# A planner that models the transfer queue, scores three tiles ahead, the mask on VectorE and the gate bias in column quarters

## The chip, the cores and the metric

One core of one Trainium2 chip runs the kernel. The metric is the device time of one execution in microseconds; of the kernel before there are three runs, median 474.86 us (474.11 to 476.41). One more execution was taken with the hardware profiler.

## The reference

Input X is 4 sequences of 1024 tokens with 256 features, all in float32. Four residual stages follow one another:

```python
x = x + attention(layernorm(x))      # causal, one head, scores / 16
x = x + ffn(layernorm(x))            # token shift, r = sigmoid, k = relu squared
x = x + state_space(x)               # own layernorm inside, gate silu(z)
x = x + ffn(layernorm(x))
# attention
Q, K, V = X @ Wq.T + bq, X @ Wk.T + bk, X @ Wv.T + bv
s = where(causal, -inf, Q @ K.T / 16);  out = softmax(s) @ V
# state_space: xz = xn @ W_in.T + b_in with xn = norm(x) * ln_g + ln_b
x_proj, z = split(xz);  z = silu(z)
B = x_proj @ W_B.T * mean(dt);  x_mean = causal convolution of B with a decay per state
y = (x_mean @ W_C.T + D_skip * x_proj) * z @ W_out.T + b_out
```

## The kernel before, in words

**Tiles.** A batch b has 8 tiles of 128 tokens; tile i = 8b + t runs over all 32. A half j = 2b + h holds four tiles, 512 tokens. Features lie in two blocks of 128 (KC = 2). Matmuls are float32, and the profile counts two instructions for each.

**Stages.** In attention every tile i has its values `pv` (L1061), its scores `sc` against all earlier tokens of the batch (L1089), a mask, the row minimum (`least`, DVE L1104; the scores carry a minus sign), the exponentials (`exponents`, ACT L1109), the turned exponentials `prT`, and the product `po` with the values (`weigh`, L1189, added to x at L1199). The mask is a bf16 matmul of an identity with a 128x128 mask into the diagonal block of the score tile, the last of the group (L1096). The first ffn (`mix1`, tag f) and the preparation of the state stage (`state_prepare`, tag h) run between the attention tiles, a batch half behind. Then come the gates of the state stage (`pz`), its inputs (`pb`), the convolution (`pc`, with sixteen shifted decay rows `hk` of 512 KB each loaded from DRAM), its outputs (`py`, `pyo`) and the second ffn (`mix2`, tag g).

**Turning.** Normalised rows have to be turned (tokens to columns). `by_dram` (L482) writes a half to DRAM (`rows_`), reads it back in four pieces (`blocks_`) and lets VectorE turn 32x32 blocks (L501); `turn_by_dram` (L1124) does it with the exponentials (`exps`, `pblocks`, L1146). Tiles with t of 0 or 1 in each batch are turned by TensorE instead (`turn`, L1158: 1 and 2 transposes into PSUM, then a copy). The first and last halves are turned by TensorE too.

**State weights.** `state_weights` (L819) multiplies W_in with ln_b for the gate bias: `pb_all`, 8 matmuls of one column each (L827), then adds b_in (L833), scales W_in by ln_g, and so on, in three steps in iterations 20 to 22.

**The order of the work.** The kernel sets the order of every engine by itself. TensorE's order is that of the calls of `unit` in the program text: the loop over i at the end gives in iteration i the scores of tile i+2, the values of i+3, first and second parts of the ffn, and `po` of tile i. All other work is given to class `Order` (L48) as `op` with a key, the keys that it needs, one or more ways (engine, cost in us, function) and a lag until its result can be used. `Order` walks along TensorE's units, keeps a model time, and as soon as an op's needs are in the model ready it goes to the offered list; the op with the earliest start, then the lowest rank, then the earliest ready time is emitted. A transfer is an op on SP (0.45 us) with a fixed lag (2.2 to 9 us), whatever else is under way. `behind(i)` (L995) is a need that holds the write of a half behind the last read of tile i's exponentials. `load(at, ...)` (L243) offers the loads of weights and tokens at a fixed model time. PSUM is two `pair` buffers (scores, `py`) and four `bank` buffers. 34 slots of SBUF are shared by most tiles.

```python
        start, _, _, n = min(
            (self._way(op)[1], op["rank"], op["time"], n) for n, op in enumerate(self.offered)
        )
```

Of the kernel before, what the change touches and what calls it, by code (L numbers as in the profile page):

```python
# [19 lines left out]
P = 128  # L20
# [16 lines left out]
RPAD = P + L  # L37
TURNED_BY_DRAM = 2
# [9 lines left out]
class Order:  # L48
# [8 lines left out]

    LAG = 0.15

    def __init__(self):  # L60
        self.now = self.at = 0.0
        self.free = {}
        self.ready = {}
        self.waiting = []
        self.offered = []
        self.psum = {"bank": [0.0] * 4, "pair": [0.0] * 2}

    def _offer(self, op):
        if all(k in self.ready for k in op["needs"]):
            op["time"] = max([self.at] + [self.ready[k] for k in op["needs"]]) + op["delay"]  # L70
            self.offered.append(op)
            return True
        return False

    def _done(self, key, time):
        if key is not None:
            self.ready[key] = time
            self.waiting = [op for op in self.waiting if not self._offer(op)]

    def _way(self, op):  # L80

        return min(
            (
                (max(op["time"], self.free.get(e, 0.0)) + c, max(op["time"], self.free.get(e, 0.0)), e, f)
                for e, c, f in op["ways"]
            ),
            key=lambda w: w[0],
        )

    def _first(self):  # L90

        if not self.offered:
            return math.inf, None
        start, _, _, n = min(
            (self._way(op)[1], op["rank"], op["time"], n) for n, op in enumerate(self.offered)
        )
        return start, n

    def _step(self):
        self.at, n = self._first()  # L100
        op = self.offered.pop(n)
        end, _, engine, emit = self._way(op)
        self.free[engine] = end
        emit()
        if op["frees"]:
            heapq.heappush(self.psum[op["frees"]], end + self.LAG)
        self._done(op["key"], end + op["lag"])

    def op(self, key, needs, *ways, frees=None, delay=0.0, lag=LAG, rank=0):

        op = dict(key=key, needs=needs, ways=ways, frees=frees, delay=delay, lag=lag, rank=rank)
        if not self._offer(op):
            self.waiting.append(op)

    def known(self, key, time):
        self._done(key, time)

    def unit(self, key, cost, needs, emit, takes=None):

        while True:  # L120
            while self._first()[0] <= self.now:
                self._step()
            missing = [k for k in needs if k not in self.ready]
            full = takes and not self.psum[takes]
            if not missing and not full:
                start = max([self.now] + [self.ready[k] for k in needs])
# [5 lines left out]
            else:  # L132
                assert self.offered, (key, missing, takes, self.psum)
# [5 lines left out]
        emit()  # L139
        self.now += cost  # L140
        self._done(key, self.now + self.LAG)

    def finish(self):
        while self.offered:
            self._step()
        assert not self.waiting
# [11 lines left out]
def hybrid_kernel(  # L158
# [84 lines left out]
    def load(at, key, *transfers, after=(), queue="SP", lag=3.0):  # L243
        o.known(f"t{at}", at)
        for k, emit in enumerate(transfers):
            last = k == len(transfers) - 1
            o.op(key if last else None, [f"t{at}", *after], (queue, 0.5, emit), lag=lag, rank=3)
# [59 lines left out]
    load(6.0, "xl2", *tokens(0, 4, 8), lag=4.0)  # L307
# [35 lines left out]

    mask_f = const.tile([P, P], F32, tag="mask_f", name="mask_f")
    make_causal_mask(nc, mask_f, MASKED)
    steps_i = const.tile([P, FINE], mybir.dt.int32, tag="steps_i", name="steps_i")
    nc.gpsimd.iota(steps_i, pattern=[[1, FINE]], base=0, channel_multiplier=0)
    mask = const.tile([P, P], BF16, tag="mask", name="mask")
    ident_b = const.tile([P, P], BF16, tag="ident_b", name="ident_b")
    steps = const.tile([P, 2, FINE], F32, tag="steps", name="steps")  # L350

    def later_constants():
        nc.vector.tensor_copy(mask, mask_f)
        nc.vector.tensor_copy(ident_b, ident)
        nc.vector.tensor_copy(steps[:, 0, :], steps_i)
        nc.vector.tensor_scalar_mul(steps[:, 1, :], steps[:, 0, :], float(FINE))
# [17 lines left out]
    def normalized(  # L374
        key, b, h, needs, dst, names, second=False, by_hand=False, after=(), spans=((0, NH),)
# [9 lines left out]
        rank = 0 if key[0] == "g" else 1  # L385
# [67 lines left out]
        for n in range(NH):  # L453
            o.op(f"{key}.st{n}", [needs[n]], ("DVE", 0.53, partial(stats, n)), rank=rank)
        for n0, n1 in spans:
# [4 lines left out]
                ("DVE", 0.08 * k, partial(variances, n0, n1)), rank=rank,  # L460
# [7 lines left out]
                ("DVE", 0.08 * k, partial(shifts, n0, n1)), rank=rank,  # L468
            )
            for n in some:  # L470
# [4 lines left out]
                    rank=rank,  # L475
                )
        parts = [f"{key}.xn{n}" for n in range(NH)]
        if not by_hand:
            by_dram(key, xn, parts + list(after), dst, names)
        return xn, parts, rs, mrs  # L480

    def by_dram(key, xn, needs, dst, names):  # L482
# [24 lines left out]
        late = 3.6 if key[0] == "g" else 5.0  # L507
        o.op(f"{key}.w", needs, ("SP", 0.45, write), lag=2.2, rank=2)
        for j in range(P // GRP):
            o.op(f"{key}.r{j}", [f"{key}.w"], ("SP", 0.45, partial(read, j)), lag=late, rank=2)  # L510
# [56 lines left out]
    class Mix:  # L567
# [4 lines left out]
        def prepare(self, j, by_hand=False, after=()):  # L572
# [9 lines left out]
                after=after,  # L582
# [59 lines left out]
        def gates(self, j, g):  # L642
            key = f"{self.tag}{j}"
            if g == 0:
# [6 lines left out]
                f"{key}.r{g}", [f"{key}.pr{g}"],  # L651
# [5 lines left out]
        def values(self, j, g):  # L657
# [24 lines left out]
            def store():  # L682
# [3 lines left out]
                f"{key}.rv{g}", [f"{key}.r{g}", f"{key}.pv{g}"], ("DVE", dve(HALF), gate),  # L686
# [3 lines left out]
            if last:  # L690
                o.op(None, [f"{key}.x{g}"], ("SP", 0.45, store), rank=3)

        def last_values(self, j, n, d0, d1):
# [12 lines left out]
            def finish():  # L706
# [11 lines left out]
                None, [f"{key}.r{n // 2}", f"{key}.pv{n}.{d0}"], ("DVE", 2 * dve(d1 - d0), finish),  # L718
# [56 lines left out]
    def decay_table():  # L775
# [29 lines left out]
        for q in range(4):  # L805
            o.op(f"r{q}", ["dec"], ("SP", 0.8, partial(write, q)), rank=3)
# [3 lines left out]
    load(40.0, None, partial(nc.sync.dma_start, r_dram[:, :P], zeros))  # L810
# [8 lines left out]
    def state_weights():  # L819
# [3 lines left out]

        def biases():
            for e in range(2 * KC):
                for c in range(KC):
                    nc.tensor.matmul(  # L827
                        pb()[:, e : e + 1], lhsT=w_in[:, c, ts(e, P)], rhs=lnb[:, c : c + 1],
                        start=(c == 0), stop=(c == KC - 1),
                    )  # L830

        def add_biases():
            nc.vector.tensor_add(b_all, pb()[:, : 2 * KC], bin_c)  # L833
# [8 lines left out]
        o.unit("pb_all", 2.0, ["w_in", "ln", "bin", "dsk"], biases, "bank")  # L842
        o.op("b_all", ["pb_all"], ("DVE", 0.2, add_biases), frees="bank")
# [11 lines left out]

        o.unit("pt_wx", 4 * TURN, ["w_in0", "w_in1"], turn, "bank")
# [138 lines left out]
    def behind(i):  # L995


        if not 0 <= i < NB * NT:
            return []
        return [f"e{i}.r{P // GRP - 1}" if i % NT >= TURNED_BY_DRAM else f"e{i}"]  # L1000

    xa_rows, xa, q, v, pr, prT, sums = {}, {}, {}, {}, {}, {}, {}

    def attend_prepare(j, by_hand=False):
# [5 lines left out]
            after=behind(NH * j - 5), spans=((0, 2), (2, NH)) if j == 0 else ((0, NH),),  # L1010
        )

    def attend_transpose(j, spans=((0, NH),)):
# [4 lines left out]
        for n0, n1 in spans:  # L1018
            for c in range(KC):
                def emit(c=c):  # L1020
# [54 lines left out]
    def scores(i):  # L1075
# [4 lines left out]
        qh, vh, keys = q[2 * b + h], v[2 * b + h], [xa[2 * b + k] for k in range(h + 1)]  # L1080
# [4 lines left out]
        def emit():  # L1085
            for k in range(h + 1):
                w = min(HALF, nk - k * HALF)
                for c in range(KC):
# [5 lines left out]
                        stop=(c == KC - 1 and k < h),  # L1094
                    )
            nc.tensor.matmul(sc()[:, ts(t, P)], lhsT=ident_b, rhs=mask, start=False, stop=True)  # L1096
# [550 lines left out]
```

## Time and profile before

| what | value |
|---|---|
| runs of the kernel, median (range) | 474.86 us (474.11 to 476.41) |
| the profiled execution's own time | 476.57 us |
| its span, first to last instruction | 474.8 us |
| mean granted clock of TensorE | 0.999 |
| instructions in the profile | 6474 |
| DMA | 68.24 MB, mean 144 GB/s |
| PE matmul po (L1189), sc (L1089) | 67.9 us, 67.2 us |
| DVE row minimum (L1104), turned exponentials (L1146) | 25.6 us, 21.7 us |

The span is what the trace covers; the execution's own time is 1.8 us longer. Busy times are unions of intervals. Matmuls are pipelined, so that their durations overlap; the distance from one start to the next tells what one costs. The line numbers are those of the kernel before.

### The profile page before, as it was taken

Reading aid. Unit: us, or ns where it says so; the run is one execution under the profiler, and the core shown is the slowest. Engines: PE = TensorE matmul, PEld = TensorE weight load, DVE = VectorE, ACT = ScalarE, POOL = GpSimd, SP = SyncE. Lnnn points to the kernel's source line nnn. Section 1 sums busy time; section 2 is a strip of 40 time slices with the busy share of each in tenths; the row PEclk is TensorE's granted clock in tenths of the full one; section 3 lists DMA queues with packets and bytes.
Section 4 is the critical chain, followed back from the end, with each engine's and each line's share of the span. In section 5 each row is a group of like instructions: output and inputs, shape, how many; then the busy total and the mean of one; then the engine's idle time right before and its main releaser. Section 6 shows DMA issues by size and latency. Waiting matters only on the chain.

```text
span 474.8 us, 6474 instructions
## 1 busy us (share of the span) xinstructions
PE 468.3 (99%) x2114; PEld 320.4 (67%) x2114; DVE 319.2 (67%) x856; ACT 190.2 (40%) x346; POOL 110.6 (23%) x119
## 2 busy tenths in 40 slices
PE   8999999999999999999999999999999999999996
PEld 5766676765866766866758766465565774877765
DVE  4657677698798797794986875410669794986312
ACT  3431435343346244344354385501113643535332
POOL 3020103101603304422223245300002210233330
PEclk9999999999999999999999999999999999999999
DMA  7649677634833944817249494902122706126112
GB/s 205 200 106 270 198 182 169 182 100 129 253 65 106 278 133 133 242 32 218 69 143 284 162 253 123 330 4 63 50 89 76 212 22 177 46 72 195 45 66 66
DMA packets 78289, 68.24 MB, mean 144 GB/s; under 512 B 13536, under 2 KB 75952, under 8 KB 78256
## 3 DMA queue, kind: packets, MB, share of 16 engines
q1 hardware_dynamic: 77440, 67.57, 48.9%
q8 instruction: 16, 0.26, 0.2%
q10 hardware_dynamic: 816, 0.26, 0.2%
q14 instruction: 17, 0.14, 0.1%
HBM read 39.95 MB, written 27.86 MB: 143 GB/s over the span
## 4 chain that ended last, share of the span: by engine, by line
PE 78%; DVE 10%; DMA 6%; SPq 3%; issue 2%; POOL 0%; ACT 0%; DVEq 0%; ACTq 0%
PE po L1189 8%; PE sc L1089 8%; PE py L1394 6%; PE pv L1061 3%; DMA pblocks<-exps 2%; DMA exps<-pr 2%; SPq L1141 2%; PE pc L1347 2%; DMA blocks_f<-rows_f 1%; PE dust L899 1%; DVE pr L1104 1%; DVE prT L1146 1%; PE py L1406 1%; SPq L495 1%; DVE hT_f L501 1%
## 5 line engine op out<-in xcount | busy, mean ns | idle before, releaser
L1189 PE MATMUL po<-v,prT 128*128 128x256 f32 x288 | 67.9, 380 | 0.5 <-DVE prT L1146 0.5
L1089 PE MATMUL sc<-xa,q 128*128 128x512 f32 (+3 forms) x192 | 67.2, 486 | 0.0
L1189 PEld LDWEIGHTS po<-v,prT 128*128 128x128 f32 x288 | 54.1, 189 | 11.0 <-issue 2.1
L1109 ACT ACTIVATE pr<-pr,nmx 128x128 f32<-128x128 f32 (+7 forms) x32 | 24.8, 774 | 71.9 <-DVE pr L1104 66.5
L1089 PEld LDWEIGHTS sc<-xa,q 128*128 128x128 f32 x192 | 35.1, 190 | 23.4 <-issue 18.9
L1061 PE MATMUL pv<-wv,xa 128*128 128x257 f32 x128 | 33.5, 384 | 0.0
L680 POOL TENSOR_TENSOR x<-x,r_f 128x512 f32<-128x512 f32 x16 | 22.5, 1410 | 40.0 <-DVE r_f L674 40.0
L427 POOL TENSOR_TENSOR rs_h<-ve_h,minus_half 128x8 f32<-128x8 f32 x8 | 13.2, 1646 | 78.1 <-DVE ve_f L414 38.9
L1104 DVE TENSOR_SCALAR_CACHE_REDUCE pr<-sc,v 128x128 f32<-128x128 f32 (+7 forms) x32 | 25.6, 799 | 7.0 <-PE sc L1096 6.8
L1146 DVE STREAM_TRANSPOSE prT<-pblocks 128x384 f32<-128x384 f32 (+5 forms) x24 | 21.7, 905 | 10.7 <-DMA pblocks<-exps 10.7
L1394 PE MATMUL py<-xnT,wk 128*128 128x512 f32 x64 | 28.8, 595 | 0.0
L1061 PEld LDWEIGHTS pv<-wv,xa 128*128 128x128 f32 x128 | 23.2, 191 | 8.0 <-issue 4.8
L680 POOL TENSOR_TENSOR x<-x,r_g 128x512 f32<-128x512 f32 x14 | 18.9, 1355 | 35.2 <-DVE r_g L674 34.2
L1234 POOL TENSOR_TENSOR x<-x,bout_r 128x512 f32<-128x512 f32 x16 | 20.2, 1274 | 26.8 <-ACT x L1227 17.7
L427 POOL TENSOR_TENSOR rs_g<-ve_g,minus_half 128x4 f32<-128x4 f32 x8 | 8.4, 1045 | 74.5 <-DVE ve_g L414 74.5
L1416 DVE SCALAR_TENSOR_TENSOR z<-py,b_skip,z 128x512 f32<-128x512 f32 x16 | 10.9, 743 | 21.6 <-PE py L1406 21.6
L1199 DVE SCALAR_TENSOR_TENSOR x<-po,rsm,x 128x256 f32<-128x256 f32 x32 | 15.5, 483 | 14.3 <-PE po L1189 11.2
L1394 PEld LDWEIGHTS py<-xnT,wk 128*128 128x128 f32 x64 | 12.0, 190 | 13.7 <-issue 13.5
L595 ACT ACTIVATE xk_g<-hT_g,muk 128x512 f32<-128x512 f32 x16 | 10.6, 712 | 20.3 <-DVE hT_g L501 20.3
L595 ACT ACTIVATE xk_f<-hT_f,muk 128x512 f32<-128x512 f32 x16 | 10.7, 714 | 19.7 <-DVE hT_f L501 11.8
L1227 ACT ACTIVATE x<-x,mrs_h,rs 128x256 f32<-128x256 f32 x32 | 17.5, 588 | 0.0
L1071 DVE TENSOR_TENSOR v<-pv,bv_r 128x257 f32<-128x257 f32 x32 | 13.2, 412 | 4.4 <-PE pv L1061 4.0
(431 smaller groups left out, 948.7 us busy)
## 6 DMA issues: line engine op xcount, KB each, us to landing
hk<-r_dram SPq DMA_DIRECT2D x16, 512.0 KB, 8.9
rows_g<-xn_g SPq DMA_DIRECT2D x8, 512.0 KB
blocks_g<-rows_g SPq DMA_DIRECT2D x32, 128.0 KB, 2.7
x<-in_L_attn_a_X_dram SPq DMA_DIRECT2D x7, 512.0 KB, 4.3
rows_f<-xn_f SPq DMA_DIRECT2D x7, 512.0 KB
blocks_f<-rows_f SPq DMA_DIRECT2D x28, 128.0 KB, 2.7
rows_h<-xn_h SPq DMA_DIRECT2D x7, 512.0 KB, 4.4
blocks_h<-rows_h SPq DMA_DIRECT2D x28, 128.0 KB, 3.0
```

Of the source, the lines that this page charges most:

```text
L427: nc.gpsimd.tensor_tensor(rs()[:, :k].rearrange("p k n -> p (k n)"), ve()[:, :k].rearrange("p k n -> p (k n)"), minus_half[:, : k * NH], A ...
L595: nc.scalar.mul(t()[:, c, :], hT()[:, c, 1:], mu[:, c : c + 1])
L680: nc.gpsimd.tensor_add(xg, xg, r()[:, ts(g, 2), :])
L1061: nc.tensor.matmul(pv()[:, : D + 1], lhsT=xaj()[:, c, ts(n, P)], rhs=wv[:, c, :], start=(c == 0), stop=(c == KC - 1),)
L1089: nc.tensor.matmul(sc()[:, k * HALF : k * HALF + w], lhsT=qh()[:, c, ts(n, P)], rhs=keys[k]()[:, c, :w], start=(c == 0), stop=(c == KC - 1 ...
L1104: nc.vector.tensor_scalar(dst, src, vh()[:, n, D : D + 1], None, ALU.add, ALU.min, accum_out=nmx(),)
L1109: nc.scalar.activation(p()[:, :nk], p()[:, :nk], AF.Exp, bias=nmx(), scale=-1.0, accum_out=sm())
L1146: nc.vector.transpose(dst()[:, : NH * width].rearrange("p (k m a) -> p k m a", m=NH, a=GRP), blocks().rearrange("p m (k a) -> p k m a", a= ...
L1189: nc.tensor.matmul(po()[:, :D], lhsT=src()[:, ts(n, P)], rhs=v[2 * b + n // NH]()[:, n % NH, :D], start=(n == 0), stop=(n == t),)
L1227: nc.scalar.activation(xt, xt, AF.Identity, bias=mrs()[:, 0, n : n + 1], scale=rs1()[:, n : n + 1])
L1234: nc.gpsimd.tensor_add(xg, xg, bout_r.unsqueeze(1).to_broadcast([P, 2, D]))
L1394: nc.tensor.matmul(dst()[:, ts(e, HALF)], lhsT=w_x[:, c, ts(e, P)], rhs=src()[:, c, :], start=(c == 0), stop=False,)
```

## The change

*Planner.* `op`, `unit`, `known` and `take` only write to a log. `finish` first works out a due time for every entry, backwards from TensorE's units (`_due`, `_backwards`), then walks along the log as before. Among ops with the same start the one that is due first goes first; ranks and `behind` are gone. A transfer names its work (`moves`, from `move(size, run)`); one queue in the model serves all transfers in turn, and a transfer is not emitted more than 30 us (HOLD) before it is due, nor long before the queue can take it. Loads have due times as well; the four `hk` of a group, the writes of `m` and the loads are separate or weighted entries.

*Scores ahead.* From iteration 4 on the loop gives the scores of tile i+3 and the values of i+4, and the queries of a half one iteration earlier.

*Turning.* Only tiles 0 and 1 of the first batch are turned by TensorE; tiles 0 and 1 of the other three go through DRAM.

*Mask.* The bf16 matmul is gone; VectorE adds a float32 mask to the diagonal block in PSUM ahead of the row minimum. The two bf16 casts at the start are gone.

*Gate bias.* ln_b is spread over 32 columns by GpSimd and is the stationary side; four matmuls, one for each quarter of the columns, run per feature block and leave four groups of equal rows; the rows are copied to SBUF, and one transpose, an iteration later, turns them to columns.

The core of the diff:

```diff
+    FLIGHT, LANDING = 1.2, 0.24
+    HOLD = 30.0
+    SHARE, MARGIN, FRONT = 0.2, 2.5, 12.0
...
+    def _enter(self, n):
+        e = self.log[n]
+        for k in e["needs"]:
+            if k not in self.ready:
+                self.waiting.setdefault(k, []).append(n)
+                return
+        time = max([self.at] + [self.ready[k] for k in e["needs"]]) + e["delay"]
+        slack = self.due[n] - time if self.FRONT < time and self.due[n] < math.inf else 0.0
+        time += max(0.0, min(self.MARGIN, self.SHARE * slack))
+        if e["moves"] and self.due[n] < math.inf:
+            time = max(time, self.due[n] - self.HOLD)
+        self.offered.append((time, n))
...
+        if self.log[n]["moves"]:
+            time = max(time, self.queue - self.FLIGHT - 0.5)
...
-            (self._way(op)[1], op["rank"], op["time"], n) for n, op in enumerate(self.offered)
+            (self._way(time, n)[1], self.due[n], time, k)
+            for k, (time, n) in enumerate(self.offered)
...
+            for k, work in enumerate(e["moves"]):
+                issued = end - (len(e["moves"]) - 1 - k) * self.log[n]["cost"] / len(e["moves"])
+                self.queue = max(self.queue, issued + self.FLIGHT) + work
+            self._done(e["key"], self.queue + self.LANDING)
...
+def move(size, run, write=False):
+    return size / run * (17 + run * (0.025 if write else 0.056)) / 16e3
...
-        late = 3.6 if key[0] == "g" else 5.0
-        o.op(f"{key}.w", needs, ("SP", 0.45, write), lag=2.2, rank=2)
+        size = 4 * P * NH * D
+        o.op(f"{key}.w", needs, ("SP", 0.47, write), moves=[move(size, 1024, True)])
...
         def biases():
-            for e in range(2 * KC):
-                for c in range(KC):
+            for c in range(KC):
+                for e in range(2 * KC):
                     nc.tensor.matmul(
-                        pb()[:, e : e + 1], lhsT=w_in[:, c, ts(e, P)], rhs=lnb[:, c : c + 1],
-                        start=(c == 0), stop=(c == KC - 1),
+                        pb()[e * GRP : (e + 1) * GRP, :P], lhsT=lnb_w()[:, c, :],
+                        rhs=w_in[:, c, ts(e, P)], start=(c == 0), stop=(c == KC - 1),
                     )
+        def turn_biases():
+            nc.tensor.transpose(pt_b()[:, :P], b_rows(), ident)
...
-            nc.tensor.matmul(sc()[:, ts(t, P)], lhsT=ident_b, rhs=mask, start=False, stop=True)
         def least():
+            diagonal = sc()[:, ts(t, P)]
+            nc.vector.tensor_add(diagonal, diagonal, mask)
             dst, src = p()[:, :nk], sc()[:, :nk]
-            if t >= TURNED_BY_DRAM:
+            if i >= TURNED_BY_DRAM:
...
     for i in range(-2, NI):
         first, second = mix_units(i)
-        if i + 2 < NI:
-            scores(i + 2)
-            if (i + 2) % NT >= TURNED_BY_DRAM:
-                turn_by_dram(i + 2)
+        while scored < min(i + (2 if i < AHEAD_FROM else 3), NI - 1):
+            scored += 1
+            scores(scored)
+            if scored >= TURNED_BY_DRAM:
+                turn_by_dram(scored)
...
-            if k == 1:
+            if k == (1 if i < AHEAD_FROM else 0):
                 both(queries, j)
-        if i + 3 < NI:
-            values(i + 3)
+        while valued < min(i + (3 if i < AHEAD_FROM else 4), NI - 1):
+            valued += 1
+            values(valued)
```

## The prediction

> **What bounds the kernel now.** I read the page first, part 1 and the clock and VectorE rows of part 2.
>
> ```profile
> PE 468.3 (99%) x2114; PEld 320.4 (67%) x2114; DVE 319.2 (67%) x856; ACT 190.2 (40%) x346; POOL 110.6 (23%) x119
> ...
> PEclk9999999999999999999999999999999999999999
> ```
>
> TensorE (PE) has work in 99% of the span at a clock of 0.9 or more in every slice; VectorE (DVE) is 67% busy, but its row of part 2, in tenths of each slice 4657677698797798794986875410669794986312, has eight slices at nine tenths or more, five of them in attention (the first 23). A busy PE may still be a waiting one, so next come the waits of PE, all that the profile shows:
>
> ```profile
> engine line waited for: us in total, times, longest us
> PE dust L899 <- DVE idle L235: 1.2, 1, 1.2
> PE pp_f2.pk L541 <- DVE xk_f L598: 0.8, 1, 0.8
> PE po L1189 <- DVE prT L1146: 0.5, 1, 0.5
> ```
>
> That is 2.5 us. As a cross-check I multiplied the instructions of the PE stream by their durations (a 512-column half of a matmul 0.43 us, a 256-column one 0.216, a 128-column transpose 0.109) and compared start with start along the timeline: of some 470 us only 9.3 are unaccounted for, 3.2 of them before 12 us, 0.72 ahead of the `po` at 44.94 and 1.01 ahead of the `pk` at 137.59. So **PE's stream is the bound**: what leaves it is gained one for one, and what the other engines do costs nothing until PE waits for it. The tail behind PE's last matmul (from 471.0 to 474.8) is not touched.
>
> **The change, part by part.**
>
> *Mask.* 32 bf16 matmuls (L1096) leave PE. Timeline of PE, start and duration, the mask and what follows it:
>
> ```profile
> 16.94 0.22 PE L1096 MATMUL sc<-mask,ident_b 128*128 128x128 bf16 x1
> 16.99 1.09 PE L1061 MATMUL pv<-wv,xa 128*128 128x257 f32 x4
> ```
>
> Durations overlap in the pipeline; what a matmul costs is the distance of the starts, here 0.05 (0.06 at 18.78, 21.11). 32 x 0.055 = **1.8 us off PE**.
>
> In its place VectorE adds a 128x128 mask in PSUM, ahead of the row minimum. No row has this form; the nearest are these (groups of VectorE by form):
>
> ```profile
> L1071 DVE TENSOR_TENSOR v<-pv,bv_r 128x257 f32<-128x257 f32 x32 | 13.2, 412 | 4.4 <-PE pv L1061 4.0
> L532 DVE COPY xm<-pc 128x128 f32<-128x128 f32 x4 | 1.2, 292 | 7.6 <-PE pc L1347 7.6
> ```
>
> The copy has the same size and also reads PSUM: 0.29 us, bounds 0.2 and 0.41. 32 x 0.29 = 9.3 us more on VectorE. It lies beside PE work, since the `pair` buffer that it holds longer is wanted only two score tiles later. If that cover goes, up to 9.3 us land on PE (rival 1).
>
> *Tiles 0 and 1 of batches 1 to 3* are turned through DRAM, as the others are. Their 9 transposes leave PE: 9 x 0.109 (eight take 0.87 us, chain of waits, `pt_a1.xa`) = **1.0 us off PE**. Added: 30 issues on SP (0.45 us each by the rows of SP), with reads of 16 and 32 KB, and 6 VectorE transposes, 0.31 and 0.44 us by the line through 384 columns in 574 ns and 1024 in 1239, for PSUM copies of 0.27 and 0.41. All of it lies beside PE's next two tiles.
>
> *Gate bias.* 16 one-column passes become 16 passes of 128 columns in four column groups that run side by side, and a transpose. Chain of waits, start, us, what:
>
> ```profile
> 173.86 1.68 PE pb_all L827 x16
> ...
> 303.74 1.85 PE pb L1289 x16
> ...
> 315.59 7.12 PE pc L1347 x256
> ```
>
> `pc` has the new form (32 rows out, 128 columns): 7.12/256 = 0.028, so 16 take 0.45. `pb` shows what entering and leaving the quarters costs: 1.85 against 4 x 0.43 = 1.72, and 0.10 more on the unit behind it (305.52 to 307.34 against 1.72). So 0.45 + 0.23 + 0.11 = 0.79, **0.9 us off PE** (bounds 0.8 and 1.1). The Trainium skill, "TensorEngine Tiling (Array Packing)", Key Properties, says that changing the tiling mode drains TensorE, which speaks against this edit. It has no price for the drain; the trace agrees, with the 0.23 us above, and by rows of a kernel without that drain the sum would be 0.2 us better. The row copy has an iteration (some 7 us) until its transpose, and that another until the bias is read, so both are covered.
>
> *Scores three ahead from tile 4 on, values and queries with them.* The order of instructions shows the same PE units otherwise. The wait at 44.94 is `po` of tile 4 for `prT`. In the new order the scores of tile 7 (3.43), the two `pp_a2` (3.44) and a `pv` (0.87) stand before it: 7.7 us more cover for a wait of 0.7. **0.7 us gained.** Of the wait at 137.59 (keys of f2) I count nothing: its blocks are now issued ahead of those of `a` and `h` instead of behind them, but on VectorE the xk of each half now stands behind a mask addition and an earlier score tile.
>
> *Planner.* It adds no instruction, it only orders VectorE, ScalarE, GpSimd and SP by due times. The largest move: the reads and writes of all seven `h` halves now stand on SP behind the exps of tile 27, where four of them used to go at 120, 152, 187 and 214 us. Weights (w_fk, w_r, w_in, w_out, w_c) go later, each still ahead of its reader by an iteration or more in the order. At the start, wk goes ahead of the first x; x tiles 2 and 3 keep third place, and the xn chain waits for them anyhow (mrs at 8.03, behind stats that start at 7.50). I cost that at nothing, bounds -0.3 (PE's gap at 10.75) and +0.5 (one issue on SP).
>
> **Sum.** 1.8 + 1.0 + 0.9 + 0.7 = 4.4. The profiled execution took 476.57 (span 474.8), which becomes 472.2 (470.4). It lies 1.7 above the median of the runs; from that median, 474.86 - 4.4 = **470.5 us**.
>
> **The rivals.**
>
> *Rival 1: VectorE becomes the bound in attention.* Windows, busy us of each engine:
>
> ```profile
> 65.00:137.00 72.00, 71.75 (x341) 50.44 (x339) 58.29 (x161) 29.99 (x58) 15.63 (x17) 1.00 0.59 157
> ...
> 235.00:240.00 5.00, 5.00 (x19) 3.09 (x18) 4.72 (x16) 1.03 (x2) 0.00 (x0) 1.00 0.24 79
> ```
>
> The third pair is VectorE: 81% over 72 us, 94% from 235 to 240. From 17 to 270 us it is busy 194 of 253; with 9.3 and some 1.5 more it is 205 of 249. Against: 44 us stay free and the order takes work by due time. For: five of attention's slices hold no free tenth, about a quarter of the tiles. Those 8 additions are 2.3 us, which PE would wait: **472.8 us**, and the whole 9.3 would give 479.8.
>
> *Rival 2, slower: the h transfers meet the decay rows.* In the new order seven `hk` of 512 KB stand on SP ahead of the first read of h6. pb (303.67) needs xnT of h6, whose VectorE transposes ended at 299.3: 4.4 us of slack. Windows, DMA share and GB/s last:
>
> ```profile
> 275.00:280.00 5.00, 5.00 (x26) 3.90 (x25) 2.51 (x5) 4.34 (x9) 3.02 (x3) 1.00 1.01 226
> 280.00:285.00 5.00, 5.00 (x13) 2.20 (x12) 4.97 (x8) 3.57 (x6) 2.40 (x2) 1.00 1.02 308
> ```
>
> At 308 GB/s an `hk` takes 1.7 us. It decides from three of them still in flight at that moment; all seven, 11.9 us, less the slack of 4.4, cost 7.5: **478.0 us** (482 at 226 GB/s). Against: from 225 to 310 us the DMA engines are busy 53 of 85 us, and four trips of 1 MB at 313 GB/s (288 at a share of 0.92, 250 to 255 us) add 13.4, so 18 us stay free; and the seven are spread over the gates and keys of f7. The Trainium skill, "DMA: Bandwidth & Descriptors", Latency and other measured facts, puts the access to HBM at 0.2 us on average and 2 at high load, an estimate of 1.8 us more a transfer, about one `hk` of the slack. No run here shows it: reads of `h` land in 2.5 to 4.4 us.
>
> *Rival 3: the plan's order does not hold on the chip.* The PE sum comes, but the first wait stays and others replace it: 474.86 - 3.7 = 471.2, inside the forecast's own range. If instead the wait at 137.59 goes too (1.0), and the smaller gaps of 0.1 to 0.4 us with it, it is 469 or below.
>
> **How the numbers follow.** Forecast, 469 to 472.4: 0.70. Better, below 469: 0.05. Rival 1, 472.5 to 475: 0.17. Rival 2, 475 to 482: 0.08. A measurement of this kernel can tell some 0.5% (2.4 us) from no change, so faster is below 472.5: 0.75; same, with a little of rival 2: 0.18; slower, above 477.2: 0.07. The range, 468 to 475, takes in the bounds of the unknown costs (0.3 on the bias, 0.5 at the start, 3 of new waits) and leaves out rival 2 and a part of the better case.
>
> **What would show it.** Mask: PE instructions fall by 32 + 9, the `sc` lines hold no bf16 matmul, and VectorE shows 32 additions near 0.29 us. Bias: pb_all near 0.7 us. Order: no wait of `po` for prT from tile 4 on. Rival 1: PE waits for `pr` or `prT` in slices where VectorE is at nine tenths. Rival 2: PE waits at pb or pc for xnT or `hk`. The forecast is wrong if PE's waits after 12 us sum to over 3 us, or if PE's stream doesn't shrink by 3.5 to 3.9.

## The result, and the profile after

The changed kernel takes **471.94 us** (median of 7 runs, 471.23 to 473.73). The kernel before, on the same chip and with the three earlier runs counted in, takes 476.37 us (7 runs, 474.11 to 480.16). The ratio is 0.992, with a 95% interval from 0.989 to 0.995: faster by about 0.8%, with the far end of the interval just at the 0.5% that can be told from no change. The forecast was 470.5 us.

The profiled execution after took 471.39 us (span 469.2) against 476.57 (474.8) before, so the span fell by 5.6 us where the forecast said 4.4. The first line of part 4 of the page before, the shares of each engine in the chain of work that ended last:

```profile
PE 78%; DVE 10%; DMA 6%; SPq 3%; issue 2%; POOL 0%; ACT 0%; DVEq 0%; ACTq 0%
```

Part 1 of the page after, and the same line of its part 4:

```profile
PE 463.4 (99%) x2074; PEld 317.2 (68%) x2074; DVE 335.0 (71%) x886; ACT 190.6 (41%) x348; POOL 110.0 (23%) x119
...
PE 96%; DMA 1%; DVE 1%; ACT 0%; SPq 0%; issue 0%; DVEq 0%
```

TensorE (PE) has 40 matmuls less: 32 masks and 9 transposes gone, one transpose added. VectorE (DVE) is busy 15.8 us more, 9.2 of it in the mask additions. The chain is the line to read here. Before, PE made up 78% of it and VectorE, DMA and SP 19%; now PE makes up 96%. Almost nothing is left that PE waits for, as the waits of PE say as well:

```profile
engine line waited for: us in total, times, longest us
PE dust L1034 <- DVE idle L353: 1.2, 1, 1.2
PE po L1322 <- DVE prT L1275: 0.3, 1, 0.3
PE pt_wq_n L1045 <- DMA wq<-in_L_attn_a_Wq_dram: 0.2, 1, 0.2
```

Both waits of before behind the first 12 us are gone, that of the `po` at 44.94 and that of the `pk` at 137.59. The one wait of `po` that is left is at 65.18; its 16 instructions show that it is tile 7, the last of the first batch (the expectations below call it tile 8). VectorE stood idle for 1.41 us just ahead of the `prT` that this `po` waits for, until the transfer of its blocks landed:

```profile
63.88 1.25 DVE L1275 STREAM_TRANSPOSE prT<-pblocks 128x1024 f32<-128x1024 f32 x1 [1.41 <-DMA pblocks<-exps]
```

So this wait is one for a trip through DRAM, not for a VectorE that has too much to do.

The mask additions in the view of their source line (durations: lowest, median, highest, in ns):

```profile
L1227 DVE TENSOR_TENSOR sc<-sc,mask x32: 260/290/300, 17.7 to 239.0; 128x128 f32<-128x128 f32 x32
```

And a window of attention, the third pair VectorE:

```profile
65.00:137.00 72.00, 71.82 (x332) 51.05 (x333) 61.51 (x170) 25.01 (x48) 12.87 (x12) 1.00 0.55 154
```

VectorE rises from 81% to 85% of this window, and PE is idle in it for 0.2 of 72 us.

**Where the 5.6 us came from.** I set the PE instructions of each kernel at their distances from start to start, as in the prediction, and compared the sum with the timeline. PE's work falls from 460.3 to 456.5 (3.8 us) and what is unaccounted for, the *gaps* below, from 9.3 to 7.5 (1.8 us). Two gaps that went are the two waits, 0.7 and 1.0. Four came: 0.4 at the `po` at 65.18, 0.5 at the `pb` at 298.08, 0.3 behind `pb_all` and 0.3 at the start. The rest, some 1.5 us, is many small gaps, and they have one pattern. Timeline of PE in the kernel before, a mask and the units behind it:

```profile
86.48 0.22 PE L1096 MATMUL sc<-mask,ident_b 128*128 128x128 bf16 x1
86.54 1.95 PE L556 MATMUL pr_f0.pv<-w_fv,ka_f 128*128 128x256 f32 x8
88.32 1.03 PE L1061 MATMUL pv<-wv,xa 128*128 128x257 f32 x4
```

The same unit in the kernel after, with no mask ahead of it:

```profile
88.55 1.89 PE L674 MATMUL pr_f0.pv<-w_fv,ka_f 128*128 128x256 f32 x8
90.28 1.03 PE L1189 MATMUL pv<-wv,xa 128*128 128x257 f32 x4
```

Read the starts: behind a mask the eight matmuls take 88.32 - 86.54 = 1.78 us, otherwise 1.73. In the trace of before this holds for the 10 such units behind a mask, for 8 `pv` (0.93 against 0.87) and for 8 more `pr`, `pk` and `pq` (0.05 to 0.06 each): 26 units and 1.4 us. A mask therefore cost its own 0.055 and again as much in the unit behind it, 3.2 us in all and not 1.8.

The sum of the parts is then 3.2 (mask) + 1.0 (transposes) + 0.8 (bias, below) + 0.7 + 1.0 (the two waits) - 1.2 (the new gaps but the one behind `pb_all`) = 5.5 of the 5.6 us. This is the account of one pair of profiles; the medians of the runs differ by 4.4 us.

### The profile page after: what moved, and what is told of

Its sections match the earlier page's. It is cut to its first block, busy times and chain, and to the rows that moved or that the text cites. A ratio compares the mean times of both kernels' runs of the same rounds, so it can differ in the third digit from the quotient of the medians.

```text
span 469.2 us, 6471 instructions
## 1 busy us (share of the span) xinstructions
PE 463.4 (99%) x2074; PEld 317.2 (68%) x2074; DVE 335.0 (71%) x886; ACT 190.6 (41%) x348; POOL 110.0 (23%) x119
## 4 chain that ended last, share of the span: by engine, by line
PE 96%; DMA 1%; DVE 1%; ACT 0%; SPq 0%; issue 0%; DVEq 0%
PE sc L1217 13%; PE po L1322 13%; PE py L1534 6%; PE pv L1189 6%; PE pc L1484 2%; PE py L1546 1%; DMA wq<-in_L_attn_a_Wq_dram 1%; PE pb L1421 1%; PE pp_a0.pq L659 1%; PE pr_g1.pv L674 1%; PE pr_g0.pr L674 1%; PE pr_f4.pr L674 1%; PE pr_f3.pr L674 1%; PE pr_f2.pr L674 1%; PE pr_f1.pr L674 1%; PE pr_f0.pr L674 1%
## 5 line engine op out<-in xcount | busy, mean ns | idle before, releaser
L797 POOL TENSOR_TENSOR x<-x,r_g 128x512 f32<-128x512 f32 x14 | 20.1, 1432 | 51.7 <-DVE r_g L791 41.3
L543 POOL TENSOR_TENSOR rs_f<-ve_f,minus_half 128x4 f32<-128x4 f32 x8 | 8.3, 1037 | 99.3 <-DVE ve_f L530 99.3
L797 POOL TENSOR_TENSOR x<-x,r_f 128x512 f32<-128x512 f32 x16 | 20.3, 1271 | 42.9 <-DVE r_f L791 41.7
L1275 DVE STREAM_TRANSPOSE prT<-pblocks 128x384 f32<-128x384 f32 (+7 forms) x30 | 23.9, 797 | 3.2 <-DMA pblocks<-exps 3.0
```

The source lines that it names most:

```text
L543: nc.gpsimd.tensor_tensor(rs()[:, :k].rearrange("p k n -> p (k n)"), ve()[:, :k].rearrange("p k n -> p (k n)"), minus_half[:, : k * NH], A ...
L797: nc.gpsimd.tensor_add(xg, xg, r()[:, ts(g, 2), :])
L1275: nc.vector.transpose(dst()[:, : NH * width].rearrange("p (k m a) -> p k m a", m=NH, a=GRP), blocks().rearrange("p m (k a) -> p k m a", a= ...
```

## The experiments

Twelve kernels ran, one of them the kernel after once more, in three groups, each group on one chip with runs of the kernel before beside it. The kernel before took 478.11 us there in the first group, 478.79 in the second and 476.79 in the third, so kernels are compared by their ratio to it and by their spans. A ratio of one group cannot be set beside that of another to better than some 0.4%, since the kernel before differs that much between groups (why is said below, with the granted clock); within a group the medians can be compared as they are. The profile of the same kernel after gave a span of 469.2 once and 468.7 the other time, so that 0.5 us of span is no difference.

| kernel | median us | ratio to before (95%) | span | PE's gaps |
|---|---|---|---|---|
| before | 476.37 | 1 | 474.8 | 9.3 |
| after | 471.94 | 0.992 (0.989 to 0.995) | 469.2 | 7.5 |
| mask_on_pe | 474.00 | 0.991 (0.988 to 0.994) | 471.8 | 8.4 |
| planner_alone | 475.24 | 0.993 (0.991 to 0.996) | 473.7 | 8.2 |
| two_ahead | 472.20 | 0.987 (0.984 to 0.989) | 469.0 | 7.3 |
| old_planner | 488.00 | 1.020 (1.016 to 1.022) | 487.1 | 25.4 |
| after_again | 471.64 | 0.986 (0.983 to 0.989) | 468.7 | 7.0 |
| old_planner_two | 482.78 | 1.009 (1.006 to 1.012) | 479.8 | 18.1 |
| mask_twice | 473.27 | 0.989 (0.986 to 0.993) | 471.3 | 9.3 |
| no_hold | 471.79 | 0.986 (0.983 to 0.989) | 471.0 | 9.4 |
| bias_on_pe | 470.64 | 0.987 (0.984 to 0.990) | 470.0 | 7.3 |
| turn_on_pe | 471.80 | 0.989 (0.986 to 0.992) | 469.8 | 7.1 |
| x_first | 469.95 | 0.985 (0.982 to 0.988) | 468.6 | 7.0 |
| old_planner_mask | 478.60 | 1.004 (1.002 to 1.006) | 476.6 | 12.9 |

The gaps are what the distances from start to start leave over, so they hold waits of PE and also work that ran slower than usual.

My theory going in was that of the prediction: PE's stream is the bound, the change is worth what leaves it, and the planner is worth next to nothing. The rivals were that VectorE limits attention, that transfers crowd, and that the planner is where the gain lies.

**mask_on_pe**: the kernel after, the mask a matmul again.

```diff
+            nc.tensor.matmul(sc()[:, ts(t, P)], lhsT=ident_b, rhs=mask, start=False, stop=True)
...
-            diagonal = sc()[:, ts(t, P)]
-            nc.vector.tensor_add(diagonal, diagonal, mask)
```

> The kernel after with the mask alone put back: 32 bf16 matmuls on TensorE, no addition on VectorE. Theory (TensorE's stream is the bound, one for one): 32 x 0.055 = 1.8 us slower than the kernel after, so 2.1 us faster than before, ratio 0.9955; the profile's span near 471.0, waits of TensorE as in the kernel after. Rival (VectorE is what counts in attention): VectorE is rid of 9.3 us, so the time is that of the kernel after or less, ratio 0.992 or below.

The span is 471.8, 2.6 to 3.1 us longer than after, with no new wait. The ratio of 0.991 falls into the range of the rival only because the kernel before took 478.11 us in this group; by the medians this kernel is 2.1 us slower than after and 1.8 us slower than two_ahead, which ran on the same chip. VectorE's 9.3 us of additions are thus hidden well enough. What the mask is worth in a whole run lies between 1.8 and 3.1 us; in the stream of PE it is worth more than the 1.8 us of its own passes: its units behind a mask again take 0.05 to 0.06 us more (10 `pv` at 0.93, 10 `pr` at 1.78), which gives 3.2.

**planner_alone**: the new planner, the other four edits undone.

> The new planner with everything else as before: mask on TensorE, tiles 0 and 1 of each batch turned by TensorE, one-column bias matmuls, scores two ahead. Theory (the gain is what left TensorE's stream, and the wait that the third tile ahead covers): TensorE's stream is that of the kernel before; of the two waits of 0.7 and 1.0 us at most the second goes, and 0.3 is lost at the start, so 473.8 to 475.2, ratio 0.997 to 1.001. Rival (the planner is the gain): most of the 3.9 us, ratio 0.992 to 0.994.

Both waits of before are gone although the scores are two tiles ahead, the mask is on PE and the stream is that of before. All that the waits of PE list is the start:

```profile
engine line waited for: us in total, times, longest us
PE dust L1020 <- DVE idle L353: 1.2, 1, 1.2
```

So the planner itself is worth 1.1 us of span, twice what two profiles of one kernel differ by. By the medians it is worth 2.9 us (478.11 to 475.24), and its runs lie within 1.2 us where those of before, on the same chip, lie within 3.7. The difference between 1.1 and 2.9 is in the profiled executions: that of before (476.57) lies 1.5 us below this median, that of planner_alone (475.57) 0.3 above its own. The ratio, 0.993, is that of the rival, and the span is that of the theory. Part of the difference is the granted clock (below): 5 of the 11 runs of before in this group have a clock of 0.996, none of planner_alone has. The median of the other six is 477.4, so that 2.2 us are left. What the longer executions of before wait for was not traced.

Why the `po` of tile 4 waited before, and does not here or in the next kernel, can be read from VectorE. First the kernel before, then two_ahead:

```profile
44.03 0.84 DVE L1146 STREAM_TRANSPOSE prT<-pblocks 128x640 f32<-128x640 f32 x1 [0.98 <-DMA pblocks<-exps]
```

```profile
41.82 0.80 DVE L1275 STREAM_TRANSPOSE prT<-pblocks 128x640 f32<-128x640 f32 x1
```

In the kernel before VectorE was idle and waited for a transfer. The four reads of `pblocks` were issued at much the same time in both kernels (37.73 to 39.19 and 37.56 to 38.86 us), but the first of them landed 5.4 us after its issue in the kernel before, and the last of them after 2.5 us in two_ahead. The kernel before issues a 512 KB load of `x` at 36.74, right ahead of these reads; two_ahead has no such load before 59.59. This speaks for the modelled queue as what removed the wait; no run tries it alone.

**two_ahead**: the kernel after, with AHEAD_FROM = 99, so that scores, values and queries are as far ahead as in the kernel before.

> The kernel after with the scores two tiles ahead all through, as before. Theory: TensorE's work is the same, only the wait of po for the turned exponentials of tile 4 comes back, 0.7 to 1.5 us, ratio 0.993 to 0.995. Rival (the third tile ahead carries the change, since the mask addition makes the way from scores to po longer): waits at many tiles, 3 us and more, ratio 0.998 and above.

The span is 469.0, as after. The third tile ahead gains nothing that can be measured. Theory and rival both fell, since each expected the waits to come back. At `po` of tile 4 there is no wait here either; at `po` of tile 7 the gap is 0.8 us instead of 0.1 to 0.6 in the kernels with three ahead, and other gaps are smaller by as much.

**old_planner**: the kernel before with the other four edits, so that only the planner is missing. Nothing in `Order` is changed.

> The kernel before, old planner and all its fixed lags, with the other four edits made: mask on VectorE, bias in quarters, tiles 0 and 1 of later batches through DRAM, scores three ahead. Theory: TensorE's stream is 3.7 us shorter and the wait of 0.7 goes, so 470 to 471.5, ratio 0.991 to 0.993, as long as the old order brings no new waits. Rival (the planner is needed, or is the gain): new waits of 2 us and more, ratio 0.996 and above.

My theory fell here: 488.0 us, 2% *slower* than before. Waits of PE:

```profile
engine line waited for: us in total, times, longest us
PE pp_f4.pk L538 <- DVE xk_f L595: 3.8, 2, 3.3
PE pp_f6.pk L538 <- DVE xk_f L595: 3.0, 1, 3.0
PE pp_a2.pq L538 <- DVE xa L498: 2.8, 1, 2.8
PE pp_a3.pq L538 <- DVE xa L498: 2.3, 1, 2.3
```

PE's stream is that of the kernel after, some 4 us shorter, yet these waits take 12 us: for the keys' input `xk_f`, and for `xa`, whose queries the third tile ahead wants an iteration earlier. The gaps are 17.9 us longer than after, so 6 more are to be explained; they come with the granted clock, below.

**after_again** and **old_planner_two** (old planner, mask, bias and turning as after, two tiles ahead) followed, to separate the third tile from the rest.

> The kernel after, unchanged, beside the other three on one chip: every theory expects 469 to 471 in the profile's span and a ratio near 0.99. The others are compared with it.

> The old planner with mask on VectorE, bias in quarters and tiles 0 and 1 through DRAM, but the scores two ahead and the queries at their old place. Theory (what broke the old order is the queries a tile earlier: their xa stood 2.6 us ahead of them before, so 8 us earlier they must wait): the waits for xa go, TensorE is 3.7 us shorter than before, time 1 to 3 us above the kernel after. Rival (the mask addition and the trips through DRAM break the fixed lags by themselves): 5 us and more above the kernel after, with waits for prT, xa or xk_f.

At two ahead the waits for `xa` are gone, but the rival held: the kernel is 11 us above after_again and still 0.9% slower than before, with one wait of 5.2 us. PE's timeline behind that wait, and the window around it (PEclk is the third number from the end):

```profile
PE pp_f2.pk L538 <- DVE xk_f L595: 5.2, 1, 5.2
...
141.29 3.75 PE L538 MATMUL pp_f2.pk<-xk_f,w_fk 128*128 128x512 f32 x4 [5.17 <-DVE xk_f L595]
144.84 1.92 PE L1076 MATMUL pv<-wv,xa 128*128 128x257 f32 x4
...
140.00:146.80 6.80, 5.51 (x9) 3.09 (x10) 4.73 (x16) 3.77 (x8) 1.01 (x1) 0.50 0.25 60
```

The wait costs more than itself. The granted clock falls to a half for 6.8 us: the four instructions of the keys take 3.55 us from start to start instead of 1.72 and those of the values 1.71 instead of 0.87, which makes 2.8 us on top of the 5.2. In old_planner there are three such stretches of 3.4 us, behind the waits of 2.3, 3.3 and 3.0 us, and they cost 5.6 us more; the wait of 2.8 us for the first `xa` was followed by none. No kernel with the new planner has one in its profile between the first 12 us and PE's last matmul.

The granted clock of the single runs bears on the kernel before. Of its 39 runs beside the experiments, 18 show a clock of 0.995 or 0.996 and take 478.1 us or more; the 21 others, at 0.998 and above, take 475.0 to 478.3. One stretch of 3.4 us at half the clock takes 0.36% off the mean clock of 476 us, which is the step from 1.000 to 0.996. By groups they are 5 of 11, 9 of 11 and 4 of 17, and so the median of before moves. Of the 60 runs of kernels with the new planner one has such a clock (mask_twice, 476.40). The profiled run of before has none, so that the spans of this document leave this part of the planner's worth out.

What VectorE did ahead of and during the wait is in its timeline (`xnT` belongs to the state stage, `xa` to attention, `hT_f` and `xk_f` to the ffn whose `pk` waits):

```profile
131.78 1.30 DVE L498 STREAM_TRANSPOSE xnT<-blocks_h 128x512 f32<-128x512 f32 x2
...
134.05 1.29 DVE L498 STREAM_TRANSPOSE xa<-blocks_a 128x512 f32<-128x512 f32 x2
...
138.69 1.30 DVE L498 STREAM_TRANSPOSE hT_f<-blocks_f 128x512 f32<-128x512 f32 x2
...
140.43 1.38 DVE L595 SCALAR_TENSOR_TENSOR xk_f<-hT_f,muk,xk_f 128x512 f32<-128x512 f32 x2
```

The same half in the kernel after:

```profile
128.88 1.31 DVE L616 STREAM_TRANSPOSE hT_f<-blocks_f 128x512 f32<-128x512 f32 x2 [0.83 <-DMA blocks_f<-rows_f]
...
130.74 1.41 DVE L715 SCALAR_TENSOR_TENSOR xk_f<-hT_f,muk,xk_f 128x512 f32<-128x512 f32 x2
132.06 1.30 DVE L616 STREAM_TRANSPOSE xa<-blocks_a 128x512 f32<-128x512 f32 x2
```

The instruction that PE needs first comes last in the old order: the transposes of the state stage, which no unit of PE needs before the first `pz` at 277.3 us, and those of `xa` stand ahead of it. The reads stood in the same order on SP (`blocks_h` from 124.0, `blocks_a` from 126.9, `blocks_f` from 132.8 us; after, `blocks_f` from 123.4 and `blocks_a` from 127.6, and no `blocks_h`). That is the old rule at work, ready first and then emitted, against due first. No run separates the order by due time from the model of the queue: they came and went together.

**mask_twice**: the kernel after with the mask added a second time, 9.3 us more on VectorE; the second addition changes no score that counts.

> The kernel after with the mask added twice, 32 more VectorE additions of 0.29 us (9.3 us), the planner's costs unchanged; the result is the same, since a masked score only gets lower. Theory (VectorE lies beside TensorE's work, with about 40 us free in attention): at most 1 us slower than the kernel after. Rival 1 (a quarter of the tiles have no free VectorE): 2.3 us slower; if all of it were on the path, 9.3.

The span grows by 2.1 to 2.6 us and the median by 1.6, so the theory's 1 us was too little; a single wait of 1.6 us, of the `po` of tile 7 for `prT`, holds most of it, with 0.6 at `pt_h7.T`. So about a quarter of a second load of this size shows. It does not show as a full VectorE: ahead of the `prT` that PE waited for, VectorE was idle for 1.52 us, until its blocks landed:

```profile
64.89 1.25 DVE L1276 STREAM_TRANSPOSE prT<-pblocks 128x1024 f32<-128x1024 f32 x1 [1.52 <-DMA pblocks<-exps]
```

The reads of these blocks were issued from 60.66, in the kernel after from 59.77; the write ahead of them (`exps`) went out at 54.70 and 54.42. So what grew is the way of the exponentials through DRAM; which part of the 0.9 us the additions caused, and how, is not shown. VectorE was busy 216 of 253 us between 17 and 270 us here, and 209 after.

**no_hold**: HOLD = 1000 instead of 30, so that transfers may go as early as the queue of the model takes them.

> The kernel after with HOLD at 1000 instead of 30 us, so that the h transfers go early, as before, and weights are loaded early. Theory (the crowded stretch from 225 to 310 us has room): within 1 us of the kernel after. Rival 2 (the held transfers meet the hk rows and cost time): 1.5 us or more faster than the kernel after. A third way: the early transfers get in front of urgent ones, 1.5 us or more slower, with waits for prT or xa.

471.79 us against 471.64 for after_again on the same chip: no difference (the profiled execution, with its span of 471.0, was the longest of the six). Under the new planner crowding of early transfers costs nothing, and the limit of 30 us gains nothing.

**bias_on_pe**: the kernel after with the one-column products back (the diff of `biases` above, reversed).

> The kernel after, with the gate bias formed by 16 one-column matmuls again instead of the four-row products in quarters of TensorE and their transpose. Theory (the sum of the matmul units): the one-column passes took 1.68 us in the trace of before, the quarters took 0.76 us from their start to the next unit in the trace of after and the transpose 0.11, so TensorE's work grows by 0.8 us; span 470.0 (the kernel after had 469.2 and 468.7), time 472.5. Rival (the quarters' switch costs what the narrow passes cost, or the transposed bias sits in a chain of its own): no growth, span 469.0, and a wait ahead of the input projection that goes when the edit is undone.

The unit takes 1.70 us from its start to the next one, against 0.76 and 0.11 for the transpose, so the edit takes 0.83 us off PE; the span is 470.0, as the theory said, 0.8 to 1.3 longer. The time did not follow: 472.5 was expected, and 470.64 is below that of after, which did not run in this group. In its own group this kernel is 0.7 us slower than x_first, which differs from the kernel after by the time of one load. The part is read from the trace alone:

```profile
177.59 0.64 PE L952 MATMUL pb_all<-w_in,lnb_w 128*32 128x128 f32 x16
178.35 1.35 PE L1322 MATMUL po<-v,prT 128*128 128x256 f32 x5
```

From the start of the quarters to the next unit are 0.76 us, for matmuls that `pc` prices at 0.44: 0.32 us more. Not all of it need be the switch. In two_ahead, no_hold, old_planner and old_planner_two the same 16 passes take 0.57 us to the next unit, 0.13 more than `pc`'s price; what holds the next unit back by another 0.19 us in the other kernels is not known. The last matmul ahead of the quarters also takes 0.09 us longer (0.52 instead of 0.43) in each of these kernels. The Trainium skill, "TensorEngine Tiling (Array Packing)", Key Properties, says that a change of the tiling mode drains TensorE. The traces agree that it costs something here, 0.13 to 0.32 us and the 0.09 ahead of it, and that this is small against the passes saved.

**turn_on_pe**: the kernel after, tiles 0 and 1 of batches 1 to 3 turned by PE again.

> The kernel after, with the first two probability tiles of batches 1 to 3 turned by TensorE again (9 transposes of 128x128 and their evictions) instead of by a trip through DRAM. Theory: the 9 transposes took 0.109 us each in the trace of before, so the work of TensorE grows by 1.0 us and nothing new waits; span 470.0, time 472.5. Rival (the trips through DRAM are paid for elsewhere: by waits of the output products for prT, 0.4 us at tile 8 in the trace of after, or by crowding of the queue): the waits for prT go when the edit is undone and the span stays at 469.2 or falls below 469.

The span is 469.8, 0.6 to 1.1 longer, with 9 transposes (1.0 us) more and no wait of `po` for `prT`. The sign is that of the theory, the size hardly above what two profiles of one kernel differ by. The median is 1.9 us above that of x_first, in the same group. The rival took the wait at 65.18 for one of the tiles that this change touches; it is of tile 7, which goes through DRAM in both kernels.

**x_first**: the load of the key weights 0.3 us later, so that the first tokens go first on SP, as before.

> The kernel after, with the load of the key weights put 0.3 us later on SP, so that the first tokens go ahead of it as in the kernel before. Theory: at the start TensorE's work on real data began at 5.02 us in the trace of after against 4.67 in that of before, and its gaps there were 0.3 us longer; the order of the first loads does that. Then the first transposes start earlier, the gaps at the start fall by 0.3 us and the span to 468.9. Rival (the start waits for the query weights on another queue, whose landing varies between executions): the first transposes start at 4.7 to 5.1 us as before and the span stays within 0.4 us of 469.2.

The rival held in its first sign, the start of the first transposes; the span lies 0.6 us below 469.2, where it allowed 0.4, but at that of after_again. The statistics of the first tokens end 0.7 us earlier (`mrs_a` at 7.51 instead of 8.22), but the first transposes of `xa` stand behind `pm_w` on PE (9.58, 9.79 after), which hangs on the query and key weights. `pt_wq_n` began at 4.86 here, at 5.02 and 4.97 in the two profiles of after and at 4.67 before. This kernel has the lowest median and ratio of all, 469.95 and 0.985, but the kernel after did not run in its group; whether it is better is open.

**old_planner_mask**: the kernel before with one edit, the mask on VectorE.

> The kernel before with one edit alone: the mask added by VectorE instead of TensorE; old planner, two tiles ahead, bias and trips through DRAM as they were. It tells which edit breaks the old planner's order. With the old planner and all three edits at two tiles ahead the span was 479.8, with 18.1 us of gaps on TensorE (9.3 in the kernel before). Theory A (the trips through DRAM break it: 6 tiles more on the queue that the old planner does not model): with the mask alone the gaps stay near 9.3, the span falls by the 1.8 us of the mask's passes to 473, and the time is 473 to 474.5. Theory B (VectorE's 9.3 us of mask adds break it, since the old planner orders VectorE by when work is ready and not by when it is due): gaps of 14 us or more with waits for xk_f or xa again, span 478 or more, time at or above that of before.

It lies between the theories: the gaps rise from 9.3 to 12.9, so that the additions alone cost the old order more than PE wins, and 0.4% slower is what is left. Some 5 us of gaps more come with the DRAM trips and the bias (old_planner_two), some 7 with the third tile ahead (old_planner). Both figures hold the stretches at half the clock, 2.8 and 5.6 us; old_planner_mask has none in its profile, but 4 of its 12 runs are at 0.993 to 0.996. The mask alone does not break the old order, and the further edits add to its cost; the bias, the trips and the third tile were not tried alone under it.

## Why the prediction was right, and where its steps were not

The bound, the direction and the size were right; the measured time lies 1.4 us above the forecast, since the forecast was taken from a median of 474.86 and all seven runs of before have 476.37, from which 4.4 us less are 472.0. The span fell by 5.6 instead of 4.4. That the size came out is in part luck: the mask was sized 1.4 us too small and a wait of 1.0 us was counted as staying, against 1.5 us of new gaps that no step had. Step by step:

- **What bounds the kernel.** Right. PE's own work fell by 3.8 us against 1.8 + 1.0 + 0.9 predicted, and nothing on another engine took it back.
- **Mask.** The mechanism was right, the size was not: 3.2 us, where the step said 32 x 0.055 = 1.8. I measured from the start of a mask to the start of the unit behind it and stopped there. The addition on VectorE was sized right (0.29 us).
- **Turning.** 1.0 us less work on PE, as predicted; undoing it costs 0.6 to 1.1 of span.
- **Bias.** 0.83 instead of 0.9: the quarters took 0.32 us beyond their passes and not 0.23; with the 0.09 ahead of them it is 0.74.
- **Third tile ahead, "0.7 us gained".** This step failed. The wait did go, but planner_alone and two_ahead are without it too, both at two tiles ahead. It was late because its blocks landed late from DRAM, with a 512 KB load issued just ahead of them; in the order of the new planner they land in time. More cover was not what it lacked. The sign named for it, no wait of `po` for `prT` from tile 4 on, holds but for tile 7.
- **The wait at 137.59, counted at nothing.** It went, 1.0 us, also in planner_alone: `blocks_f` first on SP and `hT_f`, `xk_f` first on VectorE. I had seen the first and held the mask additions against it.
- **Planner, "it adds no instruction, it only orders", costed at nothing.** Wrong as the price of that edit. Alone it is worth 1.1 us of span. And the other edits together gain only with it: without it, mask, bias and turning make the span 5.0 us longer, and with the third tile ahead 12.3 us, in which 2.8 and 5.6 us are work at half the clock. The prediction came out right because it took the edits together, and the sum of PE's stream holds only under an order that keeps PE fed.
- **The start**, bounds -0.3 and +0.5. The first product on tokens (`pp_a0.pq`) starts 0.3 us later than before in the profile of after (12.38 against 12.09), but 0.4 earlier in that of after_again (11.69), so a loss is not shown. With the loads in the old order (x_first) it starts at 12.16, between the two.
- **Rival 1** (VectorE becomes the bound) did not happen: the gaps ahead of the `po` of tile 7, 0.1 to 0.6 us with three tiles ahead, are waits for a transfer, and a second load of 9.3 us costs 2.1 to 2.6 us of span, most of it in the same wait.
- **Rival 2** (`hk` against the reads of `h`) did not happen: `xnT` of h6 ended at 292.9, 5.2 us ahead of the `pb` at 298.08, where the forecast had 4.4 us of slack to lose; the `hk` went on SP until 293.4 and landed in 8.3 us (median; 8.9 before). The gap of 0.5 there lies in `pt_h7.T`, whose eight transposes took 1.40 us instead of 1.04, and not in a transfer. The reads of `blocks_h` took 3.5 us to land, 3.0 before (the 4.4 in the prediction is the row of the writes, `rows_h`). The Trainium skill ("DMA: Bandwidth & Descriptors", Latency and other measured facts) puts the access to HBM at 0.2 us on average and 2 at high load, by which the prediction estimated 1.8 us more; the reads took 0.5 us more, and no run shows whether that is why.
- **Rival 3** was the case that touched the truth from the other side: of its better branch, the wait at 137.59 and the smaller gaps went as well, only that in this profile the start and three new gaps gave 1.5 us back.

Three things stay open: which wait brings on the stretch at half the clock in about half of the runs of before, and what else makes it vary (474.1 to 480.8) and the kernel after by 2.8 us (470.9 to 473.7); which of the loads under way sets the landing of the query weights at the start; and which part of the planner, the order by due time or the model of the queue, each wait needs.

## What to carry to other kernels

When an engine's stream is the bound, price an instruction that leaves it on both sides, by its own step and by how much shorter the same kind of unit behind it runs elsewhere in the trace. When a wait is to be removed, look at what stood ahead of the late instruction, on its engine or on the transfer queue: the new planner removed both waits here, and with it a longer lead gained nothing that can be measured. Count a wait of PE at more than its length when the clock falls behind it. And edits that load a second engine or the transfers should be tried under the order that will carry them: with the old planner the same edits made the span 12 us longer, with the new one it is 5.6 us shorter than before.

## What the runs showed of the hardware that was not expected

A single bf16 pass between float32 matmuls makes the float32 unit behind it start-to-start 0.05 to 0.06 us longer, in 26 units of the trace of before and again in the two other kernels with the mask on PE; the kernel after has none of it. The cause was not tried (the number format, the stationary identity and the narrow shape change together). And 16 passes in column quarters cost 0.13 to 0.32 us beyond their own 0.44, and 0.09 us in the matmul ahead of them.

Waits of PE of 2.3, 3.0, 3.3 and 5.2 us were followed by 3.4 or 6.8 us at half the granted clock, at 78.1, 218.1 and 272.7 us in old_planner and at 140.0 us in old_planner_two, while a wait of 2.8 us (old_planner, until 49.2) was not.
